# The products with A in the convolution's slots: two between a slot's channels and one behind them, with the normalization moved ahead

## The chip, the cores and the metric

The kernel runs on one core of one Trainium2 chip. The metric is the device time of one execution in microseconds; three runs of the kernel before gave 2986.27, 2988.52 and 2988.61 us. Engines are called PE (TensorE; PEld is its weight load), ACT (ScalarE), DVE (VectorE), POOL (GpSimd) and SP (the queue that issues DMAs).

## The reference, cut to what matters

The input is eight sequences of 2048 positions with 512 channels. Two sublayers follow each other: a state-space convolution with gelu, then a gated recurrence. The change is in the first.

```
u  = layernorm(x)                          # over the 512 channels
K  = ifft(...)                             # kernel of a 64-mode complex state space, per channel
h1 = irfft(rfft(u) * rfft(K))              # causal convolution along the 2048 positions
y  = gelu(h1 + D * u)
x  = x + layernorm(y)
# then the gated recurrence over the batch axis
c  = sigmoid(x wf' + c uf') * c + sigmoid(x wi' + c ui') * tanh(x wc' + c uc')
x  = x + layernorm(tanh(x wo' + c uo'))
```

## The kernel before, in words

The convolution isn't done with a transform. The sequence is cut into 16 chunks of 128 positions. Inside a chunk the output is a Toeplitz product (a 128x128 block `t0` for each channel); what earlier chunks leave behind is carried in a state of 128 numbers per channel and batch row, and read out by a second 128x128 block `m` for each channel. The state goes from chunk to chunk by x(j) = B u(j) + A x(j-1), with A (`at16`) and B (`bm16`) 128x128 and the same for all channels. Every operand is kept as a sum of two 16-bit halves, hi and lo, and each product is three matmuls (`mm3`, L386 to L390): hi hi, lo hi, hi lo. The function `split` (L82 to L84) takes a PSUM result apart: ACT copies it to the hi half (L83), then DVE subtracts hi to get the lo half (L84).

Channels are taken in 16 groups of 32. A loop over groups (L592) runs one block per group; I call the blocks by the group g that is convolved. Each block has 16 slots (L623). In a slot of block g, beside the convolution of two channels of group g, the work ahead for the next groups is done:

- `chain_step(g + 1, s)` (L482): the state's step for chunk s of the next group. Three matmuls with A read x(s-1), its hi half in the first two and its lo half in the third; then `split` makes x(s).
- `conv_out` (L525), in even slots: one gelu of four channels on ACT (L531).
- `conv_mm(g, s)` (L513): two channels, 12 matmuls with 128 or 120 columns.
- `tap_step` (L500), slots 1 to 12: three matmuls with 64, 128, 256 or 512 columns (two slots each of the first three widths, six of the last) that build the blocks `m` of the next group, and their `split`.
- `chain_in(g + 1, s + 1)` (L474): three matmuls with B.
- `norm_x` (L456): a part of the normalization for group g + 2. Even slots take a subtraction on POOL (L466) and a copy to u's hi half on ACT (L470), odd slots a multiplication on DVE (L468) and a subtraction on POOL for u's lo half (L472).
- `weight_split`, `weight_load` (L378, L372): in blocks 1, 2 and 14 alone, the recurrence's weights are split (ACT L383, DVE L384) or loaded in some slots.

The state's chain runs in blocks 1 to 14, where group g + 1 <= 15 is prepared. Block 0 has no chain, block 14 no normalization, block 15 (`conv_last`) neither.

The order on PE, ACT, DVE and POOL is pinned inside each block (`tc.manual_schedule`): an engine takes its instructions as the program emits them. Between blocks a planner can pull the next block's first work forward: in both programs the first product with B of the next block stands near the end of the block before. DMAs are issued on SP. PSUM has two buffers for the tap products (`pm`), three for the state (`px`), three for the outputs (`py`).

In what follows x(s), m(s), Y and U are ACT's four kinds of instruction in a slot: the hi half of the state (128x256), the hi half of the tap step (128x64 to 128x512), the gelu, and u's hi half. In a block with everything in it, ACT's order before is x, Y, m, U in an even slot and x, m in an odd one.

Of the kernel before, what the change touches and what calls it, by code (L numbers as in the profile page):

```python
# [34 lines left out]
KT = H // P  # L35
WS = (1, 4, 6, 8, 10, 11, 13, 14)  # slots in which the weights' halves are split
JF = 2  # chunks in the first part of the last group
ND1 = 3  # first slot that normalizes group 3
ND = (2, 2, 3, 3, 3, 3) + (5,) * 10  # rows of a chunk whose statistics VectorE takes (ScalarE takes the others)

# columns of the column-parameter pack
QRE, QIM, B1, B2, P1, P2, LRE, LIM, STEP, DD = range(10)
# [3 lines left out]
def s4_gated_block(ctx, tc, a, dbg=None):  # L46
# [27 lines left out]

    # long-lived results of the set-up
    at16 = kp.tile([P, 2, P], F16, name="at16")
# [20 lines left out]
    with ExitStack() as sctx:  # L97
# [9 lines left out]
        NQ = NJ  # L107
        # large temporaries sit where later tiles of the convolution will
        dri = cb.tile([P, 2, NQ, NS], F32, name="dri", tag="m", bufs=4)
# [8 lines left out]

# [1 line left out]
        stc = sp.tile([P, 1], F32, name="stc")  # L120
# [5 lines left out]

# [1 line left out]
        lre = lamb[:, None, 0:NS].to_broadcast([P, NQ, NS])  # L128
# [17 lines left out]

# [1 line left out]
        wc = sp.tile([P, 4], F32, name="wc")  # L148
# [17 lines left out]
        def cinv(out, z, n, tag):  # L166
            """out = 1 / z for tiles [n, 2, w]"""
            w = z.shape[-1]
            sq = sp.tile([n, 2, w], F32, name="sq" + tag)
            V.tensor_tensor(sq, z, z, ALU.mult)  # L170
            den = sp.tile([n, w], F32, name="den" + tag)
            V.tensor_tensor(den, sq[:, 0, :], sq[:, 1, :], ALU.add)
            V.reciprocal(den, den)
            V.tensor_tensor(out[:, 0, :], z[:, 0, :], den, ALU.mult)
            V.scalar_tensor_tensor(out[:, 1, :], z[:, 1, :], -1.0, den, ALU.mult, ALU.mult)

        def cmul(out, x, y, n, tag):
            """out = x * y (complex) for tiles [n, 2, w]"""
            w = x.shape[-1]
            t1 = sp.tile([n, 2, w], F32, name="t1" + tag, tag=f"t1_{n}_{w}")  # L180
            t2 = sp.tile([n, 2, w], F32, name="t2" + tag, tag=f"t2_{n}_{w}")
            V.tensor_tensor(t1, x, y, ALU.mult)
            V.tensor_tensor(out[:, 0, :], t1[:, 0, :], t1[:, 1, :], ALU.subtract)
            V.tensor_tensor(t2[:, 0, :], x[:, 0, :], y[:, 1, :], ALU.mult)
            V.tensor_tensor(t2[:, 1, :], x[:, 1, :], y[:, 0, :], ALU.mult)
            V.tensor_tensor(out[:, 1, :], t2[:, 0, :], t2[:, 1, :], ALU.add)

# [1 line left out]
        kc = sp.tile([P, NQ, 4], F32, name="kc")  # L189
# [38 lines left out]
        V.tensor_reduce(vv[:, 0:1], wprod, AX.X, ALU.add)  # L228
# [1 line left out]
        pq = sp.tile([2, 2, 2, NS], F32, name="pq")  # L230
# [33 lines left out]

# [1 line left out]
        omc = sp.tile([P, 2, 1], F32, name="omc")  # L266
# [11 lines left out]

# [1 line left out]
        def et(name):  # L280
# [40 lines left out]

# [1 line left out]
        mx = sp.tile([P, 2], F32, name="mx")  # L323
# [22 lines left out]

# [1 line left out]
        vs = sq16[:, LEV + 2]  # L348
# [15 lines left out]

# [1 line left out]
    WORDER = (0, 1, 2, 4, 5, 6, 3, 7)  # L366
# [19 lines left out]
    def mm3(out, w, x, start=True, stop=True):  # L386
        """out (+)= w^T x with both sides as hi + lo: hi hi + hi lo + lo hi"""
        T.matmul(out, lhsT=w(0), rhs=x(0), start=start, stop=False)  # L388
        T.matmul(out, lhsT=w(1), rhs=x(0), start=False, stop=False)  # L389
        T.matmul(out, lhsT=w(0), rhs=x(1), start=False, stop=stop)  # L390

# [1 line left out]
    yrow = {}  # L393

    def yload(q, cj, tp, sl=slice(0, H // HS)):
        """y of a chunk of block q for two steps, or some slices of it"""
        if (q, cj, tp) not in yrow:
# [6 lines left out]
    with ExitStack() as cctx:  # L404
# [4 lines left out]
        def stats(j):  # L409
            """mean and 1 / std of the rows of chunk j (VectorE and ScalarE share the batch),  # L410
            and u of the first two groups"""
            HB, nd = NB // 2, ND[j]
# [43 lines left out]
        def norm_x(g, jp, part):  # L456
            """u = LN(x) as [time, chunk, channel, batch], split in hi and lo, in four parts"""
            if g not in us or not 0 <= jp < NJ // JP:
# [15 lines left out]
        def chain_in(g, j):  # L474
            """B u of chunk j, the first part of the state after it"""
            if j == 0:
# [4 lines left out]

        def chain_step(g, j):  # L482
            x, pxt = xs_[g], pxs.pop((g, j))
            if j:
                mm3(pxt, lambda i: at16[:, i, :], lambda i: x[:, j - 1, i, :], start=False)
            split(x[:, j, 0, :], x[:, j, 1, :], pxt)

        def load_taps(g):
            """first-chunk Toeplitz blocks, and the start of the powers that read the state out"""
            for sl in (2 * g, 2 * g + 1):  # L490
# [21 lines left out]

        def conv_mm(g, c):  # L513
            """two channels of group g"""
            u, x = us[g], xs_[g]
            if c % 2 == 0:
                pys[g] = py.tile([P, 4, NJ * NB], F32, name="pyt")
            for hg in (2 * c, 2 * c + 1):
                sl, hm = 2 * g + hg // HS, hg % HS
                t0, m = t0s[sl], ms[sl]  # L520
                o = pys[g][:, hg % 4, :]
                mm3(o, lambda i: t0[:, i, :, hm], lambda i: u[:, :, i, hg, :], stop=False)
                mm3(o[:, NB:], lambda i: m[:, i, :, hm], lambda i: x[:, :, i, hg * NB : (hg + 1) * NB], start=False)

        def conv_out(g, c4):  # L525
            """gelu of four channels"""
            h4 = c4 * 4 % HS
# [8 lines left out]
        def conv_last(g):  # L536
            """the last group in two parts of the sequence: the first positions can go on earlier"""
            u, x = us[g], xs_[g]
# [41 lines left out]
        pctx.close()  # L580
        # when the weights' halves are split and loaded: {group: {slot: (splits, loads)}}
        wa = [(w, k, 0) for w in WORDER[:2] for k in (0, 2)]
# [9 lines left out]
        for g in range(NG):  # L592
# [16 lines left out]
            with tc.manual_schedule(engines=MAN):  # L609
# [13 lines left out]
                for s_ in range(NJ):  # L623
                    if g == NG - 2 and s_ == 11:
                        for cj in range(2):
                            yload(0, cj, 0, slice(0, 2 * g))
                    if ahead and s_ < NJ - 1:
                        chain_step(g + 1, s_)
                    if s_ % 2 == 0 and s_:
                        conv_out(g, s_ // 2 - 1)  # L630
                    conv_mm(g, s_)
                    if ahead and 1 <= s_ <= 12:
                        tap_step(*taps[s_ - 1])
                    if ahead and s_ < NJ - 2:
                        chain_in(g + 1, s_ + 1)
                    if nn:
                        # the loads of group 3 come late: its parts are taken in fewer slots
                        d = ND1 if g == 1 else 0
                        while norms and s_ >= d and (s_ == NJ - 1 or len(norms) > 4 + 2 * NJ * (NJ - 1 - s_) // (NJ - d)):
                            norm_x(g + 2, *norms.pop(0))  # L640
                    if g in wjobs:
# [7 lines left out]

# [1 line left out]
    FT = ctx.enter_context(tc.tile_pool(name="ft", bufs=2, reuse_waits="tile"))  # L651
# [4 lines left out]
    def lnstat(src, tag):  # L656
        """mean and 1 / std of the rows of each [P, ...] view in src"""
        n = len(src)
# [15 lines left out]
    def prep(q, t, cjs=(0, 1)):  # L674
        """x1"""
        for cj in cjs:
# [15 lines left out]
    def norm(q, t, cjs=(0, 1)):  # L692
        """its normed rows"""
        x1 = [x1s.pop((q, t, cj)) for cj in cjs]
# [4 lines left out]
    def turn(q, t, cjs=(0, 1)):  # L699
        """the normed rows with channels on partitions, split in hi and lo"""  # L700
        if (q, t) not in xts:
# [10 lines left out]
    def scan(q, t, mr=range(KT)):  # L712
        """a step of the recurrence for a block of positions"""
        xt = xts[q, t]
# [32 lines left out]
    def zbank(q):  # L747
        """a PSUM bank of products with positions on partitions (after the scan its banks are free)"""
        if q < NQB - 1:
# [110 lines left out]
def _arrays(d):  # L860
    """The inputs, laid out as the kernel reads them (copies and reorderings only)."""
    g = lambda n: np.asarray(d[n], dtype=np.float32)
# [36 lines left out]
```

## Time and profile before

| | |
|---|---|
| median of the three runs | 2988.52 us |
| span of the profiled execution (first to last instruction) | 2986.2 us |
| nearest run, the lowest | 2986.27 us |
| the stage with the change, 158 to 620 us of the span | 462 us |
| in it: PE busy, ACT busy, DVE busy, POOL busy | 419.1, 389.2, 301.8, 307.2 us |
| mean granted PE clock in it | 0.98 |
| the stage behind it (recurrence), 643 to 2986 us | 2343 us, PE busy 2325.8 |

The page gives the profiled execution no time of its own beside its span; the span is within 0.1 us of the lowest run and 2.3 us under the median. In the views, a line names the start in us, the duration, the engine, the line of the kernel, the operation, what it writes and reads, and in brackets how long the engine stood idle before it and for whom.

### The profile page before, as it was taken

How to read it: one execution, taken by the hardware profiler on the slowest of the kernel's cores; microseconds unless marked ns; L12 is line 12 of the kernel's file. 1: busy time of each engine (PE TensorE's matmuls, PEld its weight loads, DVE VectorE, ACT ScalarE, POOL GpSimd, SP SyncE). 2: the span in 40 equal slices, each digit the busy share in tenths (PEclk: the TensorE clock that was granted, in tenths of full speed). 3: DMA queues.
4: the chain of work that ended last, by engine and by line, in shares of the span. 5: the costliest groups of instructions: out<-in, count | busy, mean ns of one | idle time of the engine just before them, and what ended most of it. 6: DMA issues, size and time to landing. Idle time of an engine off the chain costs nothing.

```text
span 2986.2 us, 59439 instructions
## 1 busy us (share of the span) xinstructions
PE 2844.7 (95%) x25044; PEld 2346.3 (79%) x25044; DVE 1670.0 (56%) x3674; ACT 1130.7 (38%) x2288; POOL 730.1 (24%) x723
## 2 busy tenths in 40 slices
PE   3589999899999999999999999999999999999998
PEld 2367777788888888788888888887888788888884
DVE  7766666656645555655555555555555655563336
ACT  8888888842222222222222222222222222222221
POOL 5757777600100111111111111111111111110013
PEclk9699999989999999999999999999999999999999
DMA  8977676765522222322232222222222322221003
GB/s 223 280 216 213 204 214 202 203 174 127 107 50 58 71 72 71 78 71 72 71 93 71 72 72 72 71 72 71 72 71 72 85 72 71 71 79 43 29 29 103
DMA packets 520916, 311.32 MB, mean 104 GB/s; under 512 B 282310, under 2 KB 442568, under 8 KB 520648
## 3 DMA queue, kind: packets, MB, share of 16 engines
q1 hardware_dynamic: 520216, 306.99, 38.8%
q8 instruction: 196, 3.21, 0.5%
q14 instruction: 72, 0.59, 0.1%
q10 hardware_dynamic: 432, 0.52, 0.1%
HBM read 206.28 MB, written 101.19 MB: 103 GB/s over the span
## 4 chain that ended last, share of the span: by engine, by line
PE 71%; issue 10%; ACT 6%; DVE 5%; DMA 3%; POOL 2%; POOLq 0%; SPq 0%; ACTq 0%; DVEq 0%
PE pfi L390 12%; PE pfi L388 12%; PE pfi L389 12%; PE pgg L388 6%; PE pgg L389 6%; PE pgg L390 6%; PE pz L389 3%; PE pz L390 3%; PE pz L388 3%; ACT u L470 2%; ACT y L531 2%; PE pt L708 2%; PE pxt L390 1%; DVE xg L468 1%; PE pyt L389 1%
## 5 line engine op out<-in xcount | busy, mean ns | idle before, releaser
L389 PEld LDWEIGHTS <-w 128*128 128x128 f16 x5808 | 568.0, 98 | 73.4 <-issue 6.4
L388 PEld LDWEIGHTS <-w 128*128 128x128 f16 x5808 | 568.0, 98 | 72.3 <-issue 0.7
L390 PEld LDWEIGHTS <-w 128*128 128x128 f16 x5808 | 568.0, 98 | 72.1
L388 PE MATMUL pfi<-xt,w 128*128 128x256 f16 x2048 | 559.8, 273 | 0.7 <-ACT xt L83 0.7
L389 PE MATMUL pfi<-xt,w 128*128 128x256 f16 x2048 | 559.9, 273 | 0.0
L390 PE MATMUL pfi<-xt,w 128*128 128x256 f16 x2048 | 559.6, 273 | 0.1
L388 PE MATMUL pfi<-ch,w 128*128 128x256 f16 x1792 | 489.1, 273 | 5.1 <-ACT ch L742 5.1
L390 PE MATMUL pfi<-ch,w 128*128 128x256 f16 x1792 | 489.0, 273 | 0.1
L389 PE MATMUL pfi<-ch,w 128*128 128x256 f16 x1792 | 489.1, 273 | 0.0
L731 ACT ACTIVATE gate<-pfi,bias 128x256 f32<-128x256 f32 x512 | 214.8, 471 | 644.0 <-PE pfi L390 643.3
L737 DVE SCALAR_TENSOR_TENSOR a<-gate,cd 128x256 f32<-128x256 f32 x224 | 118.1, 527 | 508.5 <-ACT gate L731 508.5
L667 POOL TENSOR_TENSOR rsh<-rsh,nhalf 128x2 f32<-128x2 f32 (+1 forms) x65 | 45.1, 693 | 1458.6 <-DVE rsh L666 1436.4
L742 ACT ACTIVATE ch<-cd 128x256 f16<-128x256 f32 x256 | 106.6, 416 | 530.6 <-DVE cd L741 530.6
L388 PE MATMUL pgg<-xt,w 128*128 128x256 f16 x1024 | 279.1, 273 | 0.0
L389 PE MATMUL pgg<-xt,w 128*128 128x256 f16 x1024 | 279.1, 273 | 0.0
L390 PE MATMUL pgg<-xt,w 128*128 128x256 f16 x1024 | 279.1, 273 | 0.0
L389 PE MATMUL pgg<-ch,w 128*128 128x256 f16 x896 | 244.3, 273 | 0.0
L388 PE MATMUL pgg<-ch,w 128*128 128x256 f16 x896 | 244.3, 273 | 0.0
L390 PE MATMUL pgg<-ch,w 128*128 128x256 f16 x896 | 244.2, 273 | 0.0
L83 ACT ACTIVATE xt<-pt 128x512 f16<-128x512 f32 x128 | 75.8, 597 | 316.6 <-PE pz L390 218.6
L779 POOL TENSOR_TENSOR x1r<-x1r,h 128x512 f32<-128x512 f32 x124 | 181.2, 1480 | 41.1 <-DVE h L778 41.1
L740 DVE SCALAR_TENSOR_TENSOR gate<-gate,gate 128x256 f32<-128x256 f32 x256 | 108.9, 426 | 137.4 <-ACT gate L731 137.4
(303 smaller groups left out, 5964.2 us busy)
## 6 DMA issues: line engine op xcount, KB each, us to landing
xs<-in_xr SPq DMA_DIRECT2D x32, 1024.0 KB, 8.5
t<-kpad SPq DMA_DIRECT2D x32, 1024.0 KB, 5.3
xr<-in_r SPq DMA_DIRECT2D x128, 256.0 KB, 3.4
x_d<-x SPq DMA_DIRECT2D x128, 256.0 KB, 3.5
x1r<-x_d SPq DMA_DIRECT2D x128, 256.0 KB, 3.4
out<-x1r SPq DMA_DIRECT2D x128, 256.0 KB, 2.0
y<-y_d SPq DMA_DIRECT2D x62, 512.0 KB, 5.6
y_d<-y SPq DMA_DIRECT2D x30, 1024.0 KB, 6.4
```

What stands on the lines that cost most here:

```text
L83: S.activation(hi, src, AF.Copy)
L388: T.matmul(out, lhsT=w(0), rhs=x(0), start=start, stop=False)
L389: T.matmul(out, lhsT=w(1), rhs=x(0), start=False, stop=False)
L390: T.matmul(out, lhsT=w(0), rhs=x(1), start=False, stop=stop)
L470: S.activation(u[:, js, 0], xv, AF.Copy)
L531: S.activation(y[:, :, h4 : h4 + 4].rearrange("p c h -> p h c"), pys[g], AF.Gelu, scale=unsc)
L708: T.transpose(pt[:, k], xn[:, k * P : (k + 1) * P], ident)
L731: S.activation(r, outs[gt], AF.Tanh, scale=gsc[gt], bias=bs[:, gt, m : m + 1])
L737: V.scalar_tensor_tensor(a2, gate[0], 1.0, cst_[q, t - 1, m], ALU.add, ALU.mult)
L740: V.scalar_tensor_tensor(gate[1], gate[1], 1.0, gate[2], ALU.add, ALU.mult)
L742: S.activation(ch[:, 0], cd, AF.Copy, scale=0.5)
L779: (V if (q, t) >= (NQB - 1, NB - 2) else Q).tensor_tensor(x1r, x1r, hv[cj], ALU.add)
```

## The change

In each slot the gelu and the normalization's part come first. Then one channel is convolved (6 matmuls), then come the two products with A that read x(s-1)'s hi half, then the second channel, then the third product, which reads the lo half, and `split`. The tap step, the products with B and the weights follow as before.

```
-        def chain_step(g, j):
+        def chain_hi(g, j):
+            if j:
+                for i in range(2):
+                    T.matmul(pxs[g, j], lhsT=at16[:, i, :], rhs=xs_[g][:, j - 1, 0, :], start=False, stop=False)
+        def chain_lo(g, j):
             x, pxt = xs_[g], pxs.pop((g, j))
             if j:
-                mm3(pxt, lambda i: at16[:, i, :], lambda i: x[:, j - 1, i, :], start=False)
+                T.matmul(pxt, lhsT=at16[:, 0, :], rhs=x[:, j - 1, 1, :], start=False, stop=True)
             split(x[:, j, 0, :], x[:, j, 1, :], pxt)
...
-        def conv_mm(g, c):
+        def conv_mm(g, hg):
...
-                    if ahead and s_ < NJ - 1:
-                        chain_step(g + 1, s_)
                     if s_ % 2 == 0 and s_:
                         conv_out(g, s_ // 2 - 1)
-                    conv_mm(g, s_)
+                    if nn:
+                        d = ND1 if g == 1 else 0
+                        while norms and s_ >= d and (s_ == NJ - 1 or len(norms) > 4 + 2 * NJ * (NJ - 1 - s_) // (NJ - d)):
+                            norm_x(g + 2, *norms.pop(0))
+                    conv_mm(g, 2 * s_)
+                    if ahead and s_ < NJ - 1:
+                        chain_hi(g + 1, s_)
+                    conv_mm(g, 2 * s_ + 1)
+                    if ahead and s_ < NJ - 1:
+                        chain_lo(g + 1, s_)
                     if ahead and 1 <= s_ <= 12:
                         tap_step(*taps[s_ - 1])
                     if ahead and s_ < NJ - 2:
                         chain_in(g + 1, s_ + 1)
-                    if nn:
-                        d = ND1 if g == 1 else 0
-                        while norms and s_ >= d and (s_ == NJ - 1 or len(norms) > 4 + 2 * NJ * (NJ - 1 - s_) // (NJ - d)):
-                            norm_x(g + 2, *norms.pop(0))
```

The set-up's two chains, which stand outside the slots, call `chain_step` still (now the two new functions one after the other), in the same order as before.

More of the change, by code (lines that the diff above doesn't have):

```diff
@@ L480, in chain_in, with chain_step @@
             mm3(pxs[g, j], lambda i: bm16[:, i, :], lambda i: u[:, j, i, :], stop=(j == 0))
-        def chain_step(g, j):
+        def chain_hi(g, j):
[3 more added lines that the diff above has]
+        def chain_lo(g, j):
             x, pxt = xs_[g], pxs.pop((g, j))
             if j:
-                mm3(pxt, lambda i: at16[:, i, :], lambda i: x[:, j - 1, i, :], start=False)
+                T.matmul(pxt, lhsT=at16[:, 0, :], rhs=x[:, j - 1, 1, :], start=False, stop=True)
             split(x[:, j, 0, :], x[:, j, 1, :], pxt)
+        def chain_step(g, j):
+            chain_hi(g, j)
+            chain_lo(g, j)
         def load_taps(g):
@@ L511, in tap_steps @@
             return [(sl, lv, k) for lv, k in steps for sl in (2 * g, 2 * g + 1)]
-        def conv_mm(g, c):
+        def conv_mm(g, hg):
             u, x = us[g], xs_[g]
-            if c % 2 == 0:
+            if hg % 4 == 0:
                 pys[g] = py.tile([P, 4, NJ * NB], F32, name="pyt")
[L518 to L523, printed above, removed]
+            sl, hm = 2 * g + hg // HS, hg % HS
+            t0, m = t0s[sl], ms[sl]
+            o = pys[g][:, hg % 4, :]
+            mm3(o, lambda i: t0[:, i, :, hm], lambda i: u[:, :, i, hg, :], stop=False)
+            mm3(o[:, NB:], lambda i: m[:, i, :, hm], lambda i: x[:, :, i, hg * NB : (hg + 1) * NB], start=False)
         def conv_out(g, c4):
```

## The prediction

> **What bounds the kernel now.** I read the page first, then the table of stretches for the stage, then, engine by engine, the timeline of one block.
>
> ```profile
> span 2986.2 us, 59439 instructions
> PE 2844.7 (95%) x25044; PEld 2346.3 (79%) x25044; DVE 1670.0 (56%) x3674; ACT 1130.7 (38%) x2288; POOL 730.1 (24%) x723
> ```
>
> Over the whole span PE is the bound. That average is the recurrence's. The table of stretches, for 30 us inside the convolution (PE, PEld, DVE, ACT, POOL busy; clock; DMA):
>
> ```profile
> 430.00:460.00 30.00, 28.08 (x316) 23.23 (x315) 19.79 (x35) 25.90 (x44) 22.70 (x19) 1.00 0.71 212
> ```
>
> Here ACT has 25.90 of 30 us against PE's 28.08, so little must go wrong for ACT to set the beat. PE's waits, from the timeline of PE (start, duration, what; in brackets the idle time before):
>
> ```profile
> 446.39 0.27 PE L388 MATMUL pxt<-x,at 128*128 128x256 f16 x1
> 446.50 0.27 PE L389 MATMUL pxt<-x,at 128*128 128x256 f16 x1
> 447.26 0.27 PE L390 MATMUL pxt<-x,at 128*128 128x256 f16 x1 [0.49 <-DVE x L84]
> 447.37 0.22 PE L388 MATMUL pyt<-u,t 128*128 128x128 f16 x1
> ```
>
> These starts are the three products with A of one slot. Undisturbed they follow at 0.11 us; the third came 0.65 us late, for the lo half. Going through all starts of the block from 432 to 462 us, PE loses 1.2 us before the first and 2.5 us before the third products, 3.7 of its 30.18 us, and nothing noticeable elsewhere. That is what the change can win: at most some 3.7 x 11 + 22 = 63 us over the 14 blocks with a chain (11 alike, and 6.5, 5.8 and 9.9 us in blocks 1, 2 and 14).
>
> The other side is ACT's own order in the same block (x, m, Y, U by what they write):
>
> ```profile
> 432.88 0.21 ACT L83 ACTIVATE m<-pmt 128x64 f16<-128x64 f32 x1
> ...
> 435.02 0.29 ACT L83 ACTIVATE m<-pmt 128x64 f16<-128x64 f32 x1
> 435.15 1.14 ACT L470 ACTIVATE u<-xg 128x512 f16<-128x512 f32 x1
> 436.20 0.36 ACT L83 ACTIVATE x<-pxt 128x256 f16<-128x256 f32 x1
> 436.46 0.27 ACT L83 ACTIVATE m<-pmt 128x128 f16<-128x128 f32 x1
> ...
> 448.97 0.60 ACT L83 ACTIVATE m<-pmt 128x512 f16<-128x512 f32 x1 [0.61 <-PE pmt L390]
> 449.62 0.39 ACT L83 ACTIVATE x<-pxt 128x256 f16<-128x256 f32 x1
> 449.90 1.15 ACT L531 ACTIVATE y<-pyt,unsc 128x512 f32<-128x512 f32 x1
> 451.01 0.60 ACT L83 ACTIVATE m<-pmt 128x512 f16<-128x512 f32 x1
> 451.51 1.18 ACT L470 ACTIVATE u<-xg 128x512 f16<-128x512 f32 x1
> 452.57 0.39 ACT L83 ACTIVATE x<-pxt 128x256 f16<-128x256 f32 x1
> 453.24 0.60 ACT L83 ACTIVATE m<-pmt 128x512 f16<-128x512 f32 x1 [0.28 <-PE pmt L390]
> ...
> 463.06 0.20 ACT L83 ACTIVATE m<-pmt 128x64 f16<-128x64 f32 x1
> ```
>
> ACT takes its work in order: x at 436.20 starts when U lets it, though its third product had begun at 434.98. Before, Y stands between x and m, and U between m and the next x. Between an m and the next x stands one long instruction at most.
>
> **The change, part by part.** No instruction is added or removed; all durations stay. Three things move.
>
> *The third product goes behind six matmuls.* They take 0.37 us (twelve ran from 435.09 to 435.83), so third-product waits up to 0.37 us vanish: of the 2.5 us, 2.1. If that were all, the gain were 2.1 x 11 = 23 us.
>
> *x(s) starts later in the slot.* It needs the third product, now behind the slot's twelve convolution matmuls (0.74 us). Its consumer, the next slot's first product, also went back, by 0.37 us.
>
> *Y and U go ahead of x in the even slots.* This is the costly part. On ACT the order becomes Y, U, x, m in an even slot s and x, m in the odd one. Nothing lets Y start before m(s-1), which stands ahead of it and waits for the tap products of slot s-1. So there is a loop over two slots: m(s-1), Y, U, x(s), first products of slot s+1, six matmuls, third product, tap(s+1), m(s+1).
>
> Its pieces, start to next start: m 0.13, 0.20, 0.31, 0.50 for 64, 128, 256, 512 columns (435.02 to 435.15; 438.60 to 438.80; 442.27 to 442.58; 451.01 to 451.51); Y 0.93 (434.09 to 435.02); U 1.05 (435.15 to 436.20). So x(s) starts 1.98 us after m(s-1) has made room. Then x itself 0.38, to PE 0.05 (436.56 to 436.61), two products 0.22, six matmuls 0.37: 1.02 from x(s) to the third product. From there, 0.11 to the first tap matmul, 0.43 to the third, 0.42 until m starts (448.55 to 448.97): 0.96 for 512 columns; 0.11 + 0.22 + 0.31 = 0.64 for 256. For 128 columns m waits for x(s+1) instead: 0.31 (449.31 to 449.62) and 0.28, together 0.59.
>
> From the m of one odd slot to that of the next: slots 1 to 3, 0.13 + 1.98 + 1.02 + 0.59 = 3.72; 3 to 5, 0.20 + 1.98 + 1.02 + 0.64 = 3.84; 5 to 7, 0.31 + 1.98 + 1.02 + 0.96 = 4.27; 7 to 9 and 9 to 11, 0.50 + 1.98 + 1.02 + 0.96 = 4.46 each. Sum 20.75 us. Before, 432.88 to 453.24, it is 20.36. So in these slots the loop takes back all that PE was to win and 0.39 us more.
>
> *From slot 11 to slot 1 of the next block.* The program's order on ACT is m(11), Y, U, x(12), m(12), x(13), Y, U, x(14), x(0'), U, Y, x(1'), m(1'), the dash marking the next block. With m(11) at 0: x(12) at 2.48; third product of slot 13 at 3.50, x(13) at 3.81; Y 4.09, U 5.02, x(14) 6.07, x(0') 6.35. The last U needs the last DVE multiplication (L468), which now stands behind x(14)'s lo half: that starts at 6.07 + 0.38 + 0.03 = 6.48 and the multiplication 0.34 later, at 6.82. How long it takes, the trace bounds:
>
> ```profile
> 437.13 1.27 DVE L468 TENSOR_TENSOR xg<-xg,rs 128x512 f32<-128x512 f32 x1
> ...
> 460.02 0.74 DVE L468 TENSOR_TENSOR xg<-xg,rs 128x512 f32<-128x512 f32 x1 [0.61 <-POOL xg L466]
> ```
>
> ```profile
> 436.37 1.48 POOL L472 TENSOR_TENSOR u<-xg,u 128x512 f16<-128x512 f32 x1 [0.57 <-ACT u L470]
> ```
>
> Alone 0.74. At 437.13 POOL's subtraction for u had 0.72 us to go, and the multiplication took 0.53 more. In the changed order POOL's subtraction follows U's end (5.02 + 1.15) by 0.08, at 6.25, and lasts to about 7.7, 0.87 after the multiplication begins. That is nearest to the row of 437.13: 0.74 + 0.68 = 1.42, to 8.24. U at 8.28, Y 9.33, x(1') 10.26, m(1') 10.54. Before, 453.24 to 463.06: 9.82. So +0.72; with 0.74 for the multiplication +0.04. PE is not late here: its own steps reach the third product of slot 1' at about 8.6.
>
> [...]
>
> Per block 0.39 + 0.72 = +1.1 us (bounds 0.4 and 1.5, if every loop is off by 0.1 us too); eleven blocks, 3 to 13, +12.2 us.
>
> *Blocks 1, 2 and 14.* Block 14 has no U, so the loop is 1.05 us shorter and PE runs ahead. It has about seven third-product waits of 0.24 to 1.1 us; 0.37 off most of them is -2.3, the state's handover to slot 0' (below) gives back 0.5 to 0.8: I take -1.5 (-4 to 0; two of its waits, 2.4 and 1.3 us, follow DMAs of weights and stay). In blocks 1 and 2 each weight split (1.05 us on ACT) joins the loop where it falls in an odd slot or ahead of U, and the multiplication behind it on DVE delays x's lo half, while waits of 1.1 to 2.2 us lose 0.37: 0, with 2 us either way.
>
> *What costs nothing, and why.* Block 0: ACT's order there is the same. In odd slots the multiplication now stands ahead of x's lo half on DVE: the third product can be 0 to 0.39 us late for it (m's lo half ends 4.0 after m(s-1), multiplication to 4.7 to 5.5, x's lo half to 5.2 to 5.9; PE gets there at 5.55), but PE has 0.36 us until the next x of the loop. The new block's first state product in the convolution waits for x(14), 0.25 and 0.3 us; the loop hides it. On POOL the copies of L497 change places with subtractions that nobody waits for; on SP one load of xg and one of weights change places in block 1, slots ahead of their use; uncovered, that is one landing, 5.8 us.
>
> Sum: 12.2 - 1.5 = +10.7 us. Behind the stage the order on every engine is the same, PE is busy 2325.8 of 2343 us, and all of it moves. The span becomes 2986.2 + 10.7 = 2996.9; the median stood 2.3 above it: 2999 us.
>
> **Rivals.**
> - *The loop doesn't bind at the block's end.* If the last multiplication runs alone, the block gains 0.4 us only: 11 x 0.4 - 1.5 = +3, 2991.5. For it: it is two rows' difference. Against it: U ends just before. 15%.
> - *Faster.* ACT reaches x(s) early enough, and only third-product waits change: -23 and -2.3 in block 14, so 2963. It decides where Y and U together fit between m(s-1) and the third product of slot s; they need 1.98 + m, PE gives 0.33 + 0.37 + 0.22 + 0.37 = 1.3. Against it stands ACT's order in the trace. 12%.
> - *Slower still.* The multiplication ahead of x's lo half makes third products late beyond the slack, 0.35 us in six odd slots: 2.1 x 11 = +23 more, 3022. DVE's 19.8 of 30 us speaks against it. 6%.
> - *It doesn't do what it says.* The built order of PE shows the products where the diff puts them; no chance.
>
> [...]
>
> **How the numbers follow.** The forecast, 67%, has 2990 to 3006 by its bounds. Leaving out the faster and the slowest case (18%), the range is 2989 to 3008. No measurement here tells less than 0.2% (6 us) from no change. Faster 0.12; within it the first rival and the low end of the forecast, 0.18; slower 0.70.
>
> **What would show it.** Right: in a block like the one above, ACT's m(7) to m(9) at 4.4 to 4.5 us with no idle time between m, Y, U and x; PE's waits before first products in odd slots, 0.3 to 0.8 us each, on ACT x; third products nearly without waits; blocks 31.0 to 31.6 us apart. Wrong: idle time on ACT ahead of x in even slots, blocks under 30.2 us, or waits on DVE x before third products.

## The result, and the profile after

The changed kernel took 2995.70 us (median of twelve runs, 2990.97 to 2998.48), the kernel before, in runs on the same chip, 2988.14 us. The ratio is 1.0025, with a 95% interval from 1.0017 to 1.0034: slower by 5 to 10 us. The forecast was 2999 us with a range from 2989 to 3008. The span of the profiled execution went from 2986.2 to 2995.7 us.

The page's first lines, and the row of the table of stretches (PE, PEld, DVE, ACT, POOL busy; clock; DMA):

```profile
span 2995.7 us, 59428 instructions
PE 2834.9 (95%) x25044; PEld 2352.0 (79%) x25044; DVE 1657.8 (55%) x3674; ACT 1117.9 (37%) x2288; POOL 747.0 (25%) x723
...
430.00:460.00 30.00, 27.00 (x307) 23.25 (x306) 18.48 (x34) 24.42 (x42) 22.84 (x18) 1.00 0.70 211
```

In 30 us of the convolution PE has 307 matmuls where it had 316. PE, DVE and ACT are each less busy than before, and POOL is as busy (22.84 us for 22.70). So no engine got more to do: that speaks for a loop between engines, not for one full engine.

The view of waits for PE, 300 to 500 us (who, at which line, for whom: us in total, times, longest); before, then after:

```profile
PE pxt L390 <- DVE x L84: 5.6, 13, 0.5
PE pxt L388 <- ACT x L83: 4.1, 14, 0.4
```

```profile
PE pxt L486 <- ACT x L83: 17.7, 36, 1.0
PE pyt L390 <- DVE x L84: 1.3, 7, 0.2
```

L486 is the pair of first products, L492 would be the third: it has no row any more. What PE waits for now is x's hi half. By starts of matmuls PE loses 4.1 us in a block before first products (1.2 in slot 2, then 0.86, 0.65, 0.42, 0.30, 0.33, 0.37 in the odd slots), and 0.65 where the next block's convolution first reads the new state (the hand-over; the view's second row is its lo half). Before, it was 1.2 us before first and 2.5 before third products.

ACT's own order shows the loop. From the timeline of ACT, first the end of a block and the start of the next, then the stretch from one odd slot's m to that of the next odd slot:

```profile
426.34 0.60 ACT L83 ACTIVATE m<-pmt 128x512 f16<-128x512 f32 x1 [0.26 <-PE pmt L390]
...
432.41 0.73 ACT L83 ACTIVATE x<-pxt 128x256 f16<-128x256 f32 x2
434.63 1.14 ACT L470 ACTIVATE u<-xg 128x512 f16<-128x512 f32 x1 [1.49 <-DVE xg L468]
435.66 1.11 ACT L541 ACTIVATE y<-pyt,unsc 128x512 f32<-128x512 f32 x1
436.58 0.41 ACT L83 ACTIVATE x<-pxt 128x256 f16<-128x256 f32 x1
436.88 0.21 ACT L83 ACTIVATE m<-pmt 128x64 f16<-128x64 f32 x1
...
452.99 0.60 ACT L83 ACTIVATE m<-pmt 128x512 f16<-128x512 f32 x1 [0.27 <-PE pmt L390]
453.49 1.16 ACT L541 ACTIVATE y<-pyt,unsc 128x512 f32<-128x512 f32 x1
454.42 1.11 ACT L470 ACTIVATE u<-xg 128x512 f16<-128x512 f32 x1
455.39 0.41 ACT L83 ACTIVATE x<-pxt 128x256 f16<-128x256 f32 x1
...
456.74 0.38 ACT L83 ACTIVATE x<-pxt 128x256 f16<-128x256 f32 x1 [0.45 <-PE pxt L492]
457.38 0.60 ACT L83 ACTIVATE m<-pmt 128x512 f16<-128x512 f32 x1 [0.26 <-PE pmt L390]
```

From m at 452.99 to m at 457.38 it is 4.39 us. ACT has no idle time through Y, U and x. Then it waits 0.45 and 0.26 for PE, and PE had waited for that x. Neither engine is the bound alone.

At the block's end U waits 1.49 us for DVE's multiplication, and DVE and POOL, from their timelines, show why:

```profile
433.17 1.43 DVE L468 TENSOR_TENSOR xg<-xg,rs 128x512 f32<-128x512 f32 x1
```

```profile
432.59 1.45 POOL L472 TENSOR_TENSOR u<-xg,u 128x512 f16<-128x512 f32 x1 [0.69 <-ACT u L470]
```

The multiplication began 0.58 us after POOL's subtraction and took 1.43 us; the one at 460.02 in the kernel before, which began ahead of POOL's subtraction (460.18), took 0.74.

The blocks lie 31.06 us apart (by the first tap product of a block, the mean of the eleven from 248.8 to 590.4), before 30.16: +0.9 each, +9.8 in all. The rest of the span: blocks 1 and 2 are 1.7 and 1.4 us shorter, the set-up with block 0 is 0.8 longer, block 14 0.8, block 15 0.2, the recurrence 0.9. Together 9.5. (In the changed program twelve short products of block 15 stand ahead of block 14's last channels; their 0.7 us are counted with block 15.)

### The profile page after: what moved, and what is told of

It reads as the page before. It is cut to its first block, busy times and chain, and to the rows that moved or that the text cites. A ratio compares the mean times of both kernels' runs of the same rounds, so it can differ in the third digit from the quotient of the medians.

```text
span 2995.7 us, 59428 instructions
## 1 busy us (share of the span) xinstructions
PE 2834.9 (95%) x25044; PEld 2352.0 (79%) x25044; DVE 1657.8 (55%) x3674; ACT 1117.9 (37%) x2288; POOL 747.0 (25%) x723
## 4 chain that ended last, share of the span: by engine, by line
PE 68%; ACT 10%; issue 10%; DMA 4%; DVE 3%; POOL 2%; POOLq 0%; ACTq 0%; DVEq 0%; SPq 0%
PE pfi L390 12%; PE pfi L388 12%; PE pfi L389 12%; PE pgg L389 6%; PE pgg L388 6%; PE pgg L390 6%; ACT y L541 4%; ACT u L470 3%; PE pz L390 3%; PE pz L389 3%; PE pz L388 3%; PE pt L722 2%; ACT x L83 1%; DMA wl<-in_wt 1%; DMA y<-y_d 1%
## 5 line engine op out<-in xcount | busy, mean ns | idle before, releaser
L751 DVE SCALAR_TENSOR_TENSOR a<-gate,cd 128x256 f32<-128x256 f32 x224 | 109.5, 489 | 518.4 <-ACT gate L745 518.4
```

The source lines that it names most:

```text
L751: V.scalar_tensor_tensor(a2, gate[0], 1.0, cst_[q, t - 1, m], ALU.add, ALU.mult)
```

## The experiments

Each was run beside the kernel before on the same chip (2987.74 us beside the first four, 2989.87 beside the next four, 2990.26 beside the last two). In the text "the order of the change" is: gelu, normalization, channel, two products, channel, third product, tap.

### The normalization back at the slot's end (e1)

```
                     if s_ % 2 == 0 and s_:
                         conv_out(g, s_ // 2 - 1)
-                    if nn:
-                        ...
                     conv_mm(g, 2 * s_)
...
                     if ahead and s_ < NJ - 2:
                         chain_in(g + 1, s_ + 1)
+                    if nn:
+                        ...
```

> The change, with the normalization's part back at the slot's end; only U leaves its place ahead of x. Theory (ACT's loop m, Y, U, x sets the beat): with U out of it, x(s) starts 0.50 + 0.93 = 1.43 us after m(s-1) begins and its hi half reaches PE at 1.86; PE's own steps reach the next first product at 2.55, so the loop is open and PE sets the beat: 4.10 us from m(7) to m(9) (4.4 with the change), no waits inside slots 3 to 13. What stays is the block's end (x(14), the last U behind the last multiplication, then Y and x(1')): 1.2 to 1.8 us of waits. Blocks 27.7 to 28.3 us apart, 2.1 us under the kernel before, eleven times, and 4 us in blocks 1, 2 and 14: 2961 us (2952 to 2968). Rival (the new places of the products with A on PE cost the time, since the state's step ends later in the slot): the products stand as in the change, so 2993 or more, blocks 31 us apart.

Measured: 2958.57 us, ratio to the kernel before 0.9904 (0.9889 to 0.9918), span 2957.5, blocks 27.96 apart. This is faster than both kernels, and differs from the change by the place of the normalization's parts alone (U on ACT, the multiplication on DVE, the subtractions on POOL). ACT's timeline:

```profile
454.62 1.14 ACT L541 ACTIVATE y<-pyt,unsc 128x512 f32<-128x512 f32 x1
455.55 0.42 ACT L83 ACTIVATE x<-pxt 128x256 f16<-128x256 f32 x1
456.17 0.60 ACT L83 ACTIVATE m<-pmt 128x512 f16<-128x512 f32 x1 [0.20 <-PE pmt L390]
456.96 1.13 ACT L470 ACTIVATE u<-xg 128x512 f16<-128x512 f32 x1 [0.20 <-DVE xg L468]
457.99 0.36 ACT L83 ACTIVATE x<-pxt 128x256 f16<-128x256 f32 x1
```

Inside the slots one long instruction stands between any two x, Y in one slot and U in the other. PE's waits before first products shrink from 4.1 us in a block to 1.2, all of it in slot 2, and those at the hand-over from 0.65 to 0.4. What follows: the products' new places, with the gelu ahead of them, are worth about 30 us; the normalization's new place takes these back and 7 to 9 more. How the 30 us divide between the products and the gelu, e4 shows.

### The normalization alone moved ahead (e2)

The kernel before, with the normalization behind the gelu and ahead of `conv_mm`; the three products stay together at the slot's start.

> The kernel before, with the normalization's part moved ahead of the slot's convolution (ACT's order x, Y, U, m); products with A where they were. Theory: U now stands ahead of m(s), and x(s+1) starts 2.76 us after x(s) with 512 columns, 0.4 us before PE needs it; with 64 to 256 columns the first products still wait 0.3 us. The waits for lo halves stay (0.24 us each). Blocks 29.7 to 30.3 us apart: 2984 us (2978 to 2991), no clear difference. If moving U ahead is costly by itself, whatever stands around it: 2993 or more.

Measured: 2977.41 us, 0.9967 (0.9955 to 0.9979), blocks 29.47 apart: 0.6 us under the range. Ahead of the channels, but behind x, U costs nothing: ACT's order is x, Y, U, m in an even slot, and then m(s), x(s+1) with nothing long between. The waits before first products stay as in the kernel before (1.1 us a block for 1.2); those before third products, which the expectation let stay, fall from 2.5 to 1.9. So each of the two moves (in e1 the products and the gelu, here the normalization) makes the kernel before faster, by 30 and by 10 us, and both together make it slower by 7.6. It is their combination that puts both Y and U ahead of x.

### The products in their new places, ACT's order of before (e4)

The order of e1 with the gelu behind the third product; so that it reads the same four channels, it keeps the tile from ahead of `conv_mm`.

```
+                    pyt_done = pys.get(g)
...
                         chain_lo(g + 1, s_)
+                    if s_ % 2 == 0 and s_:
+                        conv_out(g, s_ // 2 - 1, pyt_done)
```

> PE's order of the change (two products between the channels, one behind), but ACT's as before: the gelu behind x, the normalization at the slot's end (x, Y, m, U). Theory: from the third product of slot s, x(s) at 0.31, Y 0.59, m(s) 1.52, U 2.02, x(s+1) 3.07, to PE at 3.50, with 512 columns; PE itself needs 3.51, so nothing waits there. With 64, 128 and 256 columns in slot s PE is ahead by 0.66, 0.5 and 0.1 us. With 1.2 us at the block's end, blocks 28.9 to 29.7 us apart, 0.9 under before: 2975 us (2968 to 2983). Rival (PE's new order costs): 2993 or more.

Measured: 2979.87 us, 0.9973 (0.9963 to 0.9982), blocks 29.5 apart, PE's waits in a block 2.6 us before first products and 0.6 at the hand-over. ACT's timeline:

```profile
449.96 0.38 ACT L83 ACTIVATE x<-pxt 128x256 f16<-128x256 f32 x1 [0.48 <-PE pxt L492]
450.24 1.18 ACT L542 ACTIVATE y<-pyt,unsc 128x512 f32<-128x512 f32 x1
451.20 0.64 ACT L83 ACTIVATE m<-pmt 128x512 f16<-128x512 f32 x1
451.73 1.13 ACT L470 ACTIVATE u<-xg 128x512 f16<-128x512 f32 x1
452.74 0.39 ACT L83 ACTIVATE x<-pxt 128x256 f16<-128x256 f32 x1
```

It is 21 us slower than e1, and only Y's place differs: now Y, m and U all stand between x(s) and x(s+1), and nothing long between x(s+1) and x(s+2). The same work on ACT is dearer when it falls into one of two slots. So of the 29 us that e1 gained on the kernel before, the products' places are worth 8, and the gelu's place ahead of them, which the change brings along, 21.

### The third product alone behind six matmuls (e5)

The kernel before, with the first two products still at the slot's start, the third between the channels, and ACT's order x, Y, m, U.

> The kernel before, with the third product alone moved behind the slot's first channel; two products at the slot's start, gelu behind x, normalization at the end (ACT's order as before). The prediction priced this move alone at 2.1 us a block, 23 us in all. Followed through, x(s) also starts 0.37 us later against the next slot's first products, which did not move back: third product of slot s at 0, x(s+1) reaches PE at 3.50 with 512 columns and PE needs it at 3.51; with 64 to 256 columns first products wait 0.66, 0.5, 0.1 us (0.57, 0.30, 0 before). So the gain is about half: blocks 28.9 to 29.5 apart, 2975 us (2965 to 2982). If the price of 2.1 us stands: 2964.

Measured: 2981.01 us, 0.9977 (0.9968 to 0.9987), blocks 29.63 apart. The third products' waits are gone, as predicted. But the waits before first products went from 1.2 to 3.2 us in a block (0.79, 0.83 and 0.65 about its start). The prediction's "2.1 x 11 = 23 us", "if that were all", was not to be had: 0.5 us a block arrived. PE had been waiting in two places for the same loop.

### The multiplication a slot earlier (e6)

The change, with the last multiplication taken in slot 14 and not in slot 15, so that it isn't queued just ahead of U.

```
-   len(norms) > 4 + 2 * NJ * (NJ - 1 - s_) // (NJ - d)
+   len(norms) > 4 - (s_ == NJ - 2) + 2 * NJ * (NJ - 1 - s_) // (NJ - d)
```

> The change, with one thing moved: the last DVE multiplication of a block's normalization (chunk pair 7) is emitted in slot 14 and not in slot 15, so it stands ahead of x(14)'s lo half and the block's last U need not wait for it. In the changed kernel that U stands idle 1.5 us for the multiplication, and Y, x(1') and m(1') follow it. Theory (this wait is a link of ACT's loop at the block's end): m(11) to m(1') falls from 10.6 to about 9.3 us, blocks 29.8 us apart, 2982 us; part may be lost where x(14)'s lo half now waits behind the multiplication (2979 to 2992). Rival (PE or the state's handover would be as late anyway): blocks stay 31 us apart, 2995.

Measured: 2989.48 us, 1.000 (0.999 to 1.0009), blocks 30.40 apart: 0.65 us a block gained of the 1.49 that U had waited. ACT's timeline shows what is late next:

```profile
458.87 0.38 ACT L83 ACTIVATE x<-pxt 128x256 f16<-128x256 f32 x1
459.13 1.18 ACT L470 ACTIVATE u<-xg 128x512 f16<-128x512 f32 x1
460.19 1.14 ACT L541 ACTIVATE y<-pyt,unsc 128x512 f32<-128x512 f32 x1
461.10 0.44 ACT L83 ACTIVATE x<-pxt 128x256 f16<-128x256 f32 x1
462.48 0.38 ACT L83 ACTIVATE x<-pxt 128x256 f16<-128x256 f32 x1 [0.94 <-PE pxt L492]
```

The five lines are x(14), U, Y, x(0') and x(1'). In the change x(0') stood right behind x(14), and U with its wait, and Y, ahead of x(1') alone. Here U doesn't wait, but U and Y now stand ahead of x(0') itself, and x(1') follows 1.38 us behind x(0'), which must first pass through PE. From x(14) to x(1') it is 3.61 us where it was 4.17, which is most of the 0.65. The wait for the multiplication was a real link of the chain, but without it the next link holds the block up: 0.84 of the 1.49 us are not won.

### Half of U (e7)

The change, with ACT copying one chunk of U and DVE the other, so that the loop's U is shorter.

```
-                S.activation(u[:, js, 0], xv, AF.Copy)
+                S.activation(u[:, j0, 0], xv[:, 0], AF.Copy)
+                V.tensor_copy(u[:, j0 + 1, 0], xv[:, 1])
```

> The change, with U cut in two: ACT copies the first chunk of the pair (256 columns, some 0.57 us), DVE the second. The order is the change's. Theory (the loop m, Y, U, x on ACT is the beat): each loop loses 0.48 us until PE's own steps bind: slots 1 to 3 3.24, 3 to 5 3.36, 5 to 7 3.8, 7 to 9 and 9 to 11 4.10, together 18.6 instead of 20.5; the block's end, with two U, 1.0 less. Blocks 28.2 us apart, 2960 us (2950 to 2970). Rival (the time went to PE's order or to DVE): DVE only has more to do, 2995 or more.

Measured: 2970.42 us, 0.9934 (0.992 to 0.9949), blocks 28.77 apart, 25 us under the change and 0.4 above the range that was expected. From m(9) to m(11) it is 4.07 us (437.03 to 441.10), where 4.10 was expected and the change has 4.39. The first products' waits in the odd slots are gone; PE loses 0.7 us in slot 2, and 1.5 before third products, for the lo half, which the expectation had not. So a shorter instruction of ACT in the loop, though DVE got more work, moved the time as the loop says. The rival, that ACT isn't in it, would have left 2995.

### Half of U where there is no such loop (e8, e9) and DVE's copy by itself (e10, e11)

e8 is e1 with the edit of e7, e9 is the kernel before with it.

> The normalization back at the slot's end as in the first experiment, and U cut in two as in the run beside this one. In the first experiment the slots wait for nothing but 1.2 us after the block's end, behind Y and two U. Theory: that wait falls by about 0.5 us a block: 2952 us (2946 to 2958), the fastest so far. If PE's own steps bound it already everywhere: 2958.

> The kernel before with U cut in two in the same way: the control. Its ACT order (x, Y, m, U) has U alone between m and the next x, so only the waits of first products behind a short tap step shrink, from 1.2 us to some 0.4 a block; the waits for lo halves (2.5 us) stay, since DVE gets 0.3 us more each pair of slots. Blocks 29.3 us apart, 2978 us (2970 to 2984): a gain of a third of what the same cut brings the change. Then the change, slower with the whole U, is faster by some 18 us with the half one.

Both expectations missed: e8 took 2966.96 us (0.9925, 0.9909 to 0.9942), 6 us slower than e1 when each is set against the kernel before on its own chip, and e9 2995.53 us (1.0019, 1.0009 to 1.0028), 6 us slower than the kernel before. The groups from 300 to 500 us show DVE's part (count | busy us, mean ns | idle before, for whom); e1, then e8:

```profile
L468 DVE TENSOR_TENSOR xg<-xg,rs 128x512 f32<-128x512 f32 x58 | 66.9, 1154 | 4.9 <-POOL xg L466 4.9
```

```profile
L468 DVE TENSOR_TENSOR xg<-xg,rs 128x512 f32<-128x512 f32 x57 | 75.0, 1317 | 0.0
L470 ACT ACTIVATE u<-xg 128x256 f16<-128x256 f32 x56 | 38.0, 679 | 22.2 <-DVE xg L468 22.2
```

In e1 ACT's U waited 7.9 us in that stretch for the multiplication, in e8 22.2. To see whether DVE's copy alone does this, e10 and e11 leave U whole on ACT and let DVE copy the half into a spare tile that nobody reads:

```
                 S.activation(u[:, js, 0], xv, AF.Copy)
+                spare = cr.tile([P, G, NB], F16, name="spare", bufs=1)
+                V.tensor_copy(spare, xv[:, 1])
```

> The version with the normalization back at the slot's end, and beside it a second copy by DVE of half of U's input into a spare tile that nobody reads; ACT's U stays whole, so DVE alone gets more work (the copy took 0.37 us alone and 0.92 to 1.19 beside POOL where it replaced half of U). Theory that DVE's extra work made the half-U version lose against 2958.6: blocks at 28.5 us or more instead of 27.96, time 2969 us (2963 to 2978), and U waits longer for DVE's multiplication. Rival, that it was another effect of ACT's shorter U, and DVE has room for 0.7 us more every second slot: 2957 to 2961, blocks at 28.0.

> The kernel before with the same spare copy by DVE, U whole. Theory that DVE's extra work ate what the half U brought in the order of before: x's lo half gets later behind a longer queue on DVE, third-product waits grow, time 3002 us (2995 to 3012), slower than the kernel before with half U (2995.5), since here ACT is not relieved. Rival, that DVE has room: 2986 to 2991, no change.

Measured: e10 2968.14 us (0.9919, 0.9902 to 0.9935), blocks 28.55 apart; e11 2997.47 us (1.0023, 1.0014 to 1.0033), blocks 30.49 apart. Against the kernel before on the same chip, e10 is 22 us faster where e1 was 29, and e11 7 slower: DVE's copy costs some 7 us in either order, as much as e8 and e9 lost, to within 1 or 2 us that these runs can't tell from nothing. In e1's order the blocks say the same: 28.55 us apart with the copy alone and with the half U, 27.96 without. The rival, that DVE has room, falls.

By which way the copy costs, the traces show in part. In e10 U waits longer for the multiplication, as expected: 12.3 us in the same 200 us. In e11 third-product waits did not grow, as had been expected: they are 2.5 us a block as before, and first-product waits went from 1.2 to 1.5. In e9 the eleven alike blocks are as long as in the kernel before (30.20 and 30.16 us): first-product waits are gone there, third-product waits are 3.8 for 2.5, and what the run lost stands in other blocks. The copies, from the timeline of e10:

```profile
435.14 0.37 DVE L472 CAST spare<-xg 128x256 f16<-128x256 f32 x1
...
452.16 1.21 DVE L472 CAST spare<-xg 128x256 f16<-128x256 f32 x1
```

The second ran while POOL was at its subtractions (449.75 to 454.75 without a pause); the first ended before POOL began one at 435.54. The lo half of an x is queued behind the second copy: it started at 453.30.

## Why the prediction was right, point by point

*The loop over two slots.* Right in kind, and in size in the narrow slots. From m to m of odd slots the block at 436.88 has 3.72, 3.83, 4.20, 4.36 and 4.39 us, where 3.72, 3.84, 4.27, 4.46 and 4.46 were predicted: 20.50 in place of 20.75. The mis-sized term is U to x: taken as 1.05 from a slot with 64 columns, it is 0.97 in the slots with 512 (454.42 to 455.39).

*The block's end.* Right to 0.02 us in its last steps: with m(11) at 426.34, U at 8.29 (8.28 predicted), Y 9.32 (9.33), x(1') 10.24 (10.26), m(1') 10.54 (10.54). The multiplication began at 6.83 (6.82) and took 1.43 (1.42). The prediction's "Alone 0.74" is no multiplication without POOL: a POOL subtraction starts at 460.18, while that one runs. It is the time of one that started first. In the row of 437.13 it is 0.55 us from POOL's end (437.85) to its own (the prediction's 0.53 is 1.27 less 0.74). Here POOL ended at 434.04 and the multiplication at 434.60, 0.56 later.

*The third product.* That its waits vanish was right; that this is worth 2.1 us a block, "if that were all", was not (e5: 0.5). The waits moved to the first products. The sum didn't need this step, since the loop overrode both.

*Eleven blocks:* +12.2 us predicted, +9.8 measured, inside the bounds of 0.4 to 1.5 each.

*Blocks 1 and 2* gained 3.1 us where 0 with 2 either way was taken. Most of it can be the clock: the granted clock is 0.95 in both blocks in the kernel before, 0.98 and 1.00 in the change, and where it was 0.50 in the kernel before (224 to 227 us) products with 256 columns follow at 0.21 us in place of 0.11. Estimated from these figures and the blocks' lengths (33 to 35 us), that is worth 2.7 us at most, if PE was never waiting while the clock was low. In block 2 the low stretch stands behind a third-product wait of 2.2 us at 223 us; the longest wait of the change there is 1.7 us. That the one brings the other was not tried.

*Block 14* is the term that failed: +0.8 us where -1.5 (-4 to 0) was taken. Its third-product waits fell as forecast, from 4.8 to 1.9 us. But "Block 14 has no U, so the loop is 1.05 us shorter and PE runs ahead" leaves out the weight splits (L383, 1.05 us each on ACT). After slots 1, 11 and 13 they stand ahead of Y and x, in the loop; the prediction counted them so in blocks 1 and 2 alone. First-product waits went from 4.4 to 8.4 us. The longest, ACT and then PE:

```profile
620.65 1.06 ACT L383 ACTIVATE w<-wl 128x1024 f16<-128x1024 f32 x1 [2.42 <-DMA wl<-in_wt]
621.61 1.11 ACT L541 ACTIVATE y<-pyt,unsc 128x512 f32<-128x512 f32 x1
622.53 0.41 ACT L83 ACTIVATE x<-pxt 128x256 f16<-128x256 f32 x1
```

```profile
622.99 0.38 PE L486 MATMUL pxt<-x,at 128*128 128x256 f16 x2 [2.27 <-ACT x L83]
```

The split waits for a DMA of weights, and with the gelu's new place x waits for the split and for Y. In the kernel before x stood ahead of Y there, and PE waited 1.09 us at the same place (613.10). Whether the change also made the weights come later stays open.

*Not in the sum:* the set-up with block 0 took 0.8 us more, block 15 0.2, the recurrence 0.9; what lengthens them was not tried. That the sum comes out at 9.5 on the span (10.7 predicted) is partly luck: these 1.9 us and the 2.3 by which block 14 missed cancel the 3.1 of blocks 1 and 2 and part of what the eleven blocks fell short. From span to time the prediction added 2.3 us, a difference between two executions; the changed kernel's profiled run took 1.8 us more than its own span (2997.51 and 2995.7).

*The rivals.* The multiplication does bind at the block's end (e6), if for 0.65 us of its 1.49. The faster case, 2963 us, is what e1 shows to be there as soon as U is out of the way (2958.6): third-product waits gone, first-product waits 1.2 us as before. The prediction had the condition right: Y and U ahead of x do not fit.

## What to carry to other kernels

On an engine that takes its work in order (as ACT here: in the change x at 455.39 started when U let it, though its third product had begun at 454.07) and feeds a recurrence, count the long instructions between one link of the chain and the next, in every slot: here one in each link (e1) beat two in every other one (the change, e4) by 37 and 21 us, with the same work on every engine. The kernel before, e2 and e5 have two in every other link as well, and none of them came within 18 us of e1. Two moves that each help can hurt together when they meet in front of the same instruction, so try them apart, and look for what a move brings along: here the gelu's place was worth more than the products'. And a wait that a reordering removes is a gain only if the loop behind it gets shorter (e5: 0.5 of 2.1 us a block): add up the loop, not the waits.

## What the runs showed that had not been expected

DVE, busy 140 of 200 us in e1, had no room for 0.7 us more in every second slot: the copy cost 0.6 us a block, some 7 us in all (e10). Its length went with what POOL did, 0.37 us alone (435.14) and 1.21 us beside POOL's subtractions (452.16), and the lo half of an x, which the chain needs, started behind it, at 453.30.

In all 90 cases of the change between 240 and 590 us in which a DVE multiplication started while a POOL subtraction ran, it ended 0.54 to 0.57 us behind that subtraction's end. That is some 0.19 us less than the 0.74 it took where it started first (460.02 in the kernel before).
